# Delta*u*B on GpSimd for some states, and tiles of one state, in a deformable-convolution plus Mamba kernel

## The chip, the cores and the metric

The kernel runs on one core of a Trainium2 chip. A core has TensorE (PE; its weight loads are listed as PEld), VectorE (DVE), ScalarE (ACT), GpSimd (POOL) and SyncE (SP), which here only issues transfers; each works through its own queue in order. On-chip memory is SBUF (128 partitions) and PSUM, which receives the results of TensorE. The metric is the device time of one execution in microseconds.

## The reference

The input is x of shape (4, 128, 128, 128): four images of 128 rows, 128 columns and 128 channels. There are two layers, each `x = x + f(group_norm(x))`.

Layer 0 is a deformable convolution. A 3x3 convolution predicts offsets, each output pixel samples nine shifted positions bilinearly for each of two channel groups, and a depthwise and a pointwise convolution follow.

Layer 1 is a stack of two Mamba blocks. Each image row is a sequence of 128 steps with 128 channels, widened to 256. For each of these 256 channels and 16 states, the block computes a recurrence along the sequence:

```
deltaA  = exp(delta * A)              # decay
deltaBu = (delta * u) * B
h_t     = deltaA_t * h_(t-1) + deltaBu_t
y_t     = sum over the 16 states of h_t * C_t
out     = (y + u * D) * silu(res) @ out_proj
```

u, delta, B and C come from projections of the sequence, a short causal convolution, silu and softplus. All of it is float32.

## The kernel before, in words

Layer 0 works image by image. `gather` issues, on GpSimd, indirect DMAs (L364) that fetch the sampled pixels from a table in device memory, with indices that lie in SBUF; there are 2304 an image. `sample` weights what they brought on DVE (gw, L382, a TENSOR_TENSOR with both inputs in SBUF), adds the samples up on TensorE and copies them to SBUF on ScalarE; `add_up` applies the combined depthwise and pointwise weights on TensorE. Gather buffers (gt) are four deep.

Layer 1 works in jobs: four image rows (`SR`), which are four sequences or 512 steps (`TB`), through one of the two Mamba blocks. An image has 32 such row groups and so 64 jobs. `pre` prepares a job: u, delta, the product du = delta*u (L547 to L550 on DVE), and B and C, which are written to device memory as rows (`bcd`). `main` runs the recurrence. The 256 channels are two halves (`NC`) of 128 partitions, so one state of one job is a tile of 128 x 2 x 512.

In `main`, a step handles two states (`NQ`), and there are eight steps:

- SP loads B and C of the two states, broadcast to all partitions, into `bc0` and `bc1`, two buffers each (L570).
- ScalarE writes zeros to the first step of each sequence in the decay tile `da` (L575), so that the scan starts afresh there, and the decays to the rest (L580, four instructions of 508 elements). There are three `da` tiles.
- DVE makes `hs` = du * B, one instruction per state (L586); then one scan over both states, 2048 elements a partition, which writes the states over the decays in `da` (L592); then the product with C in `da`, also one instruction (L596). The two products are SCALAR_TENSOR_TENSOR with a multiplication by a column of ones.
- TensorE adds the transposed 128x128 pieces into y in PSUM (L128).

After the eight steps DVE multiplies y, in PSUM, with the gate (L607), TensorE projects, and the last block's result goes out through the tile `ot` (L629 to L632).

The main loop runs the steps of layer 1 on image b together with pieces of layer 0 on image b + 1. So the first image's layer 0 runs alone, three images of layer 1 run beside gathers, and the last image of layer 1 runs alone. Each engine's queue has the order that the framework's scheduler gave it from its own estimates of durations and from the free buffers; it is fixed before the run.

Of the kernel before, what the change touches and what calls it, by code (L numbers as in the profile page):

```python
# [10 lines left out]
F32 = mybir.dt.float32  # L11
I32 = mybir.dt.int32
AF = mybir.ActivationFunctionType
ALU = mybir.AluOpType
# [3 lines left out]
P = 128  # L18
G = 2
CG = 64  # L20
NT = 9
RB = 8
SR = 4
TB = SR * P
NGT = 4
NL = 2
NC = 2
NS = 16
NQ = 2
DTR = 8  # L30
DCONV = 4
# [32 lines left out]
def block_kernel(ctx: ExitStack, tc: tile.TileContext, a: dict, out: bass.AP):  # L64
    nc = tc.nc
    x = a["x"]
    B, H, W, C = x.shape
# [21 lines left out]
    cw = ctx.enter_context(tc.tile_pool(name="w", bufs=1))  # L89
# [4 lines left out]
    p2 = ctx.enter_context(tc.tile_pool(name="l1p2", bufs=1))  # L94
# [4 lines left out]
    def loadw(name, shape, src=None, pool=cw, tag=None):  # L99
        t = pool.tile(shape, F32, name=f"w_{name}", tag=tag) if tag else pool.tile(shape, F32, name=f"w_{name}")  # L100
        nc.sync.dma_start(t, a[name] if src is None else src)
        return t
# [13 lines left out]
    ones = cw.tile([P, P], F32, name="ones")  # L116
# [5 lines left out]
    inc = cw.tile([P, NL, DCONV, NC * P], F32, name="inc")  # L122
    aneg = cw.tile([P, NL, NC, NS], F32, name="aneg")
    ddiag = cw.tile([P, NL, NC, P], F32, name="ddiag")

    def add_transposed(o, v, start, stop):

        nc.tensor.matmul(o, v, ident, is_transpose=True, start=start, stop=stop, skip_group_check=True)  # L128
# [4 lines left out]


    dw = loadw("dw", [P, NT, NT], pool=p2, tag="dbl")
    dwb = loadw("dwb", [P, NT], pool=p2, tag="ot")
    pw = loadw("pw", [P, NT, CG], pool=p2, tag="u")
    pwb = loadw("pwb", [P, 1], pool=p2, tag="w1")
    nc.vector.tensor_tensor(
# [15 lines left out]
    alog = loadw("alog", [P, NL, NC, NS], pool=p2, tag="dbl")  # L155
    nc.scalar.activation(aneg, alog, AF.Exp)
    nc.vector.tensor_scalar(aneg, aneg, -1.0, None, ALU.mult)
    dpar = loadw("dpar", [P, NL, NC], pool=p2, tag="ot")
    for l in range(NL):
        for c in range(NC):  # L160
            nc.vector.tensor_scalar(ddiag[:, l, c, :], ident, dpar[:, l, c : c + 1], None, ALU.mult)
    inw = loadw("inw", [P, NL, NC * P], a["inw"][:, :, 0 : NC * P], pool=p2, tag="yg")
    cvw = loadw("cvw", [P, NL, DCONV, NC * P], pool=p2, tag="hs")
    for l in range(NL):
        nc.vector.tensor_tensor(
            inc[:, l], cvw[:, l], inw[:, l].unsqueeze(1).to_broadcast([P, DCONV, NC * P]), ALU.mult
        )


# [289 lines left out]

    NDA = 3
    das = [cw.tile([P, NC, NQ, SR, P], F32, name=f"da{i}") for i in range(NDA)]
    zero = cw.tile([P, NC * NQ * SR], F32, name="zero")
    nc.vector.memset(zero, 0.0)
    n_da = [0]

    NH = 2
# [5 lines left out]
    def next_h():  # L474
        n_h[0] += 1
        return hps[n_h[0] % NH]

    def load_x1(blk, nm):
        b, off = divmod(blk * TB, H * W)
        t = p2.tile([P, TB], F32, tag="x1t", name=f"x1t_{nm}", bufs=2)  # L480
        nc.sync.dma_start(t, x1[b][:, off : off + TB])
        return t
# [70 lines left out]
    def main(st, l):  # L553

        blk = st["blk"]
        nm = f"{blk}_{l}"

        y = psy.tile([P, SR, NC, P], F32, tag="y", name=f"y_{nm}")
        for i in range(SR):
            for c in range(NC):  # L560
                nc.tensor.matmul(  # L561
                    y[:, i, c], st["u"][:, c, i * P : (i + 1) * P], ddiag[:, l, c, :],
                    start=(i % 2 == 0 and c == 0), stop=False, skip_group_check=True,
                )
        for q in range(NS // NQ):
            bc = []
            for w in range(2):
                t = p2.tile([P, NQ, TB], F32, tag=f"bc{w}", name=f"bc{w}_{nm}_{q}", bufs=2)
                n0 = w * NS + q * NQ
                nc.sync.dma_start(t, st["bcd"][n0 : n0 + NQ, :].partition_broadcast(P))  # L570
                bc.append(t)
            da = das[n_da[0] % NDA]
            n_da[0] += 1

            nc.scalar.copy(da.rearrange("p c n s t -> p (c n s) t")[:, :, 0], zero)  # L575
            for c in range(NC):
                dv = st["delta"][:, c].rearrange("p (s t) -> p s t", s=SR)
                for n in range(NQ):
                    s = q * NQ + n
                    nc.scalar.activation(  # L580
                        da[:, c, n, :, 1:], dv[:, :, 1:], AF.Exp, scale=aneg[:, l, c, s : s + 1]
                    )
            hs = p2.tile([P, NC, NQ, TB], F32, tag="hs", name=f"hs_{nm}_{q}")

            for n in range(NQ):
                nc.vector.scalar_tensor_tensor(  # L586
                    hs[:, :, n, :], st["du"], ones[:, 0:1],
                    bc[0][:, n].unsqueeze(1).to_broadcast([P, NC, TB]),
                    op0=ALU.mult, op1=ALU.mult,
                )  # L590
            df = da.rearrange("p c n s t -> p (c n s t)")
            nc.vector.tensor_tensor_scan(  # L592
                df, df, hs.rearrange("p c n t -> p (c n t)"), zero[:, 0:1], ALU.mult, ALU.add
            )
            dc = da.rearrange("p c n s t -> p c (n s t)")
            nc.vector.scalar_tensor_tensor(  # L596
                dc, dc, ones[:, 0:1],
                bc[1].rearrange("p n t -> p (n t)").unsqueeze(1).to_broadcast([P, NC, NQ * TB]),
                op0=ALU.mult, op1=ALU.mult,
            )  # L600
            for c in range(NC):
                for n in range(NQ):
                    for i in range(SR):
                        add_transposed(y[:, i, c], da[:, c, n, i, :], False, q == NS // NQ - 1 and n == NQ - 1)
            yield
        gt = st["g"]
        nc.vector.tensor_tensor(gt, y.rearrange("p s c d -> p s (c d)"), gt, ALU.mult)  # L607
        yg = p2.tile([P, NC, TB], F32, tag="yg", name=f"yg_{nm}")
        for c in range(NC):
            pt = ps1.tile([P, SR, P], F32, tag="t", name=f"pyg_{nm}_{c}")  # L610
            for i in range(SR):
                nc.tensor.transpose(pt[:, i, :], gt[:, i, c * P : (c + 1) * P], ident)  # L612
            nc.scalar.copy(yg[:, c], pt.rearrange("p s t -> p (s t)"))
        po = ps1.tile([P, TB], F32, tag="t", name=f"pout_{nm}")
        if l < NL - 1:
            for c in range(NC):
                nc.tensor.matmul(po, ow[:, l, c, :], yg[:, c], start=(c == 0), stop=(c == NC - 1))
            st["h"] = next_h()
            nc.scalar.copy(st["h"][:, :, DCONV - 1 :], po.rearrange("p (s t) -> p s t", s=SR))
        else:  # L620
            x1t = load_x1(blk, f"o{nm}")
            for i in range(SR):
                o = po[:, i * P : (i + 1) * P]
                nc.tensor.matmul(o, x1t[:, i * P : (i + 1) * P], ident, start=True, stop=False)
                for c in range(NC):
                    nc.tensor.matmul(
                        o, yg[:, c, i * P : (i + 1) * P], ow[:, l, c, :], start=False, stop=(c == NC - 1)
                    )
            ot = p2.tile([P, SR, P], F32, tag="ot", name=f"ot_{nm}")  # L629
            nc.scalar.copy(ot.rearrange("p r c -> p (r c)"), po)  # L630
            b, row = divmod(blk * SR, H)
            nc.sync.dma_start(out[b, row : row + SR].rearrange("r w c -> w r c"), ot)  # L632
# [8 lines left out]
    def layer1():  # L641
        pre(*jobs[0])
        for i, job in enumerate(jobs):
            if i + 1 < len(jobs):
                pre(*jobs[i + 1])
            yield from main(*job)
# [11 lines left out]
    n0 = NJ * NT  # L658
# [67 lines left out]
def build(arrays):  # L726

    import concourse.bacc as bacc

    nc = bacc.Bacc("TRN2", target_bir_lowering=False, num_devices=1)  # L730
    a = {
        k: nc.dram_tensor(f"in_{k}", v.shape, mybir.dt.from_np(v.dtype), kind="ExternalInput").ap()
        for k, v in arrays.items()
    }
    out = nc.dram_tensor("out_0", arrays["x"].shape, F32, kind="ExternalOutput").ap()
    with tile.TileContext(nc) as tc:
        block_kernel(tc, a, out)
    return nc
# [9 lines left out]
```

## Time and profile before

| | us |
|---|---|
| Time, median of 3 runs | 26701.57 (26690.43 to 26703.51) |
| The profiled execution's own time | 26698.06 |
| Its span | 26696.0 |
| DVE busy | 23505.8 (88%) |
| PE busy | 19620.5 (73%) |
| POOL busy | 16017.0 (60%) |
| ACT busy | 11605.1 (43%) |

One profiled execution is taken apart into instructions. A group line gives the kernel line, engine, operation, output tile and inputs, shapes and count; behind the bar stand total busy time in us and the mean of one in ns, then the engine's idle time just before such instructions and what ended it. L128 is a helper, so that its groups are told apart by their tiles. A line of the view by stretches has the stretch and its length, then busy time and number of instructions of each engine, the granted TensorE clock, the share of the DMA engines in use, and GB/s. A line of the timeline has the start, the duration, engine, line and operation, and in brackets the idle time before it and what ended it.

### The profile page before, as it was taken

To read this page: it belongs to the slowest core of one execution; us is meant where nothing else is said; L and a number is where in the kernel's file an instruction comes from. 1 tells how busy PE (TensorE), PEld (TensorE's weight loads), DVE (VectorE), ACT (ScalarE), POOL (GpSimd) and SP (SyncE) were. 2 spreads that over 40 slices of the span, in tenths; PEclk is the share of its full clock that TensorE was granted. 3 is DMA by queue.
4 is the path that set the end of the run, shared out by engine and by line. 5 is a ranking of instruction groups with operands and counts; after the bars stand their busy time and mean duration, and the time that the engine had idled before them with its cause. 6 is when DMAs were issued, how large, how long until landed. Compare 5 with 4: busy or idle time off the path is not lost. (4 is left out here: it accounts for less than half of the span.)

```text
span 26696.0 us, 294801 instructions
## 1 busy us (share of the span) xinstructions
PE 19620.5 (73%) x112196; PEld 13523.4 (51%) x112196; DVE 23505.8 (88%) x14042; ACT 11605.1 (43%) x18181; POOL 16017.0 (60%) x9222
## 2 busy tenths in 40 slices
PE   4777788878888778887888778888888655555555
PEld 3444455555555555555555555555555443434344
DVE  2232289999999999999999999999999999999999
ACT  0000044444444544444444454444445455555554
POOL 4777777878877767888878667877878400000000
PEclk7888888888999888888998888899998866666666
DMA  5363344456544444455544444444444333333332
GB/s 146 114 172 107 106 147 155 157 170 183 165 153 154 149 144 155 158 173 181 164 154 153 148 143 151 156 150 152 154 154 156 130 107 106 107 106 107 107 106 102
DMA packets 1994602, 3804.53 MB, mean 143 GB/s; under 512 B 771796, under 2 KB 1116116, under 8 KB 1993053
## 3 DMA queue, kind: packets, MB, share of 16 engines
q1 hardware_dynamic: 1550812, 2577.13, 29.9%
q0 software_dynamic: 442368, 1208.55, 14.4%
q8 instruction: 880, 14.42, 0.2%
q14 instruction: 542, 4.43, 0.0%
HBM read 3567.63 MB, written 217.05 MB: 142 GB/s over the span
## 5 line engine op out<-in xcount | busy, mean ns | idle before, releaser
L364 POOL DMA_INDIRECT gt<-table,idx x9216 | 16016.3, 1738 | 5031.5 <-issue 2999.5
L592 DVE TENSOR_TENSOR_SCAN da<-da,zero,hs 128x2048 f32<-128x2048 f32 x2048 | 9176.1, 4481 | 351.7 <-ACT da L580 247.1
L128 PE MATMUL y<-ident,da 128*128 128x128 f32 x32768 | 5252.0, 326 | 3956.1 <-DVE da L596 3955.4
L580 ACT ACTIVATE da<-de,aneg 128x508 f32<-128x508 f32 x8192 | 5550.5, 712 | 5605.2 <-PE y L128 5351.0
L128 PEld LDWEIGHTS y<-ident,da 128*128 128x128 f32 x32768 | 4682.4, 171 | 4953.3 <-DVE da L596 2520.6
L415 PE MATMUL acc<-s,wc 128*64 128x256 f32 (+3 forms) x38400 | 6403.2, 453 | 761.4 <-ACT s L396 760.9
L586 DVE SCALAR_TENSOR_TENSOR hs<-du,ones,bc 128x1024 f32<-128x1024 f32 x4096 | 5093.2, 1277 | 0.0
L415 PEld LDWEIGHTS acc<-s,wc 128*64 128x64 f32 x38400 | 3352.0, 145 | 3083.2 <-issue 1446.2
L596 DVE SCALAR_TENSOR_TENSOR da<-da,ones,bc 128x2048 f32<-128x2048 f32 x2048 | 4807.9, 2348 | 25.9
L382 DVE TENSOR_TENSOR gw<-gt,wt 128x1024 f32<-128x1024 f32 x2304 | 2786.4, 1213 | 2133.3 <-DMA gt<-table,idx 1500.9
L128 PE MATMUL p<-ident,gw 128*128 128x128 f32 x18432 | 2724.3, 299 | 1714.1 <-DVE gw L382 1706.7
L128 PEld LDWEIGHTS p<-ident,gw 128*128 128x128 f32 x18432 | 2292.8, 154 | 2329.3 <-DVE gw L382 1752.7
L396 ACT COPY s<-p 128x512 f32<-128x512 f32 x1152 | 668.6, 581 | 3989.8 <-PE p L128 3982.0
L501 PE MATMUL pu<-hp,inc 128*128 128x512 f32 x4096 | 1808.3, 593 | 0.0
L580 ACT ACT_TABLE_LOAD x1016 | 1303.5, 1283 | 16.8 <-PE y L128 5.7
L501 PEld LDWEIGHTS pu<-hp,inc 128*128 128x128 f32 x4096 | 751.2, 188 | 865.9 <-issue 865.2
L508 ACT ACTIVATE u<-pu,w_cvb 128x512 f32<-128x512 f32 x512 | 324.6, 684 | 1468.9 <-PE y L561 1461.4
L561 PEld LDWEIGHTS y<-ddiag,u 128*128 128x128 f32 x4096 | 579.5, 200 | 192.0 <-issue 192.0
L612 PE MATMUL pyg<-ident,g 128*128 128x128 f32 x2048 | 353.9, 328 | 425.7 <-DVE g L607 424.8
L546 ACT ACT_TABLE_LOAD x500 | 641.5, 1283 | 8.9
L561 PE MATMUL y<-ddiag,u 128*128 128x128 f32 x4096 | 612.1, 284 | 0.0
L263 PE MATMUL pof<-xn,w_offw 128*64 128x512 f32 x2304 | 585.0, 613 | 20.0 <-ACT xn L257 12.0
(118 smaller groups left out, 11036.3 us busy)
## 6 DMA issues: line engine op xcount, KB each, us to landing
bc<-bcd SPq DMA_DIRECT2D x4096, 512.0 KB
gt<-table,idx POOLq DMA_INDIRECT x9216
table<-xt SPq DMA_DIRECT2D x984, 128.0 KB
xt<-in_x SPq DMA_DIRECT2D x124, 320.0 KB
xr<-in_x SPq DMA_DIRECT2D x128, 256.0 KB
x<-xo SPq DMA_DIRECT2D x128, 256.0 KB
x1t<-x SPq DMA_DIRECT2D x128, 256.0 KB
x1t_o<-x SPq DMA_DIRECT2D x128, 256.0 KB
```

What stands on the lines that cost most here:

```text
L128: nc.tensor.matmul(o, v, ident, is_transpose=True, start=start, stop=stop, skip_group_check=True)
L364: nc.gpsimd.indirect_dma_start(out=gt[:, v, r], out_offset=None, in_=flat, in_offset=bass.IndirectOffsetOnAxis(ap=idx[:, ri, o : o + 1], a ...
L382: nc.vector.tensor_tensor(gw.rearrange("p r s v c -> p (r s) v c"), gts[h].rearrange("p v r (s c) -> p (r s) v c", c=CG), wv.unsqueeze(3). ...
L396: nc.scalar.copy(st[:, :, 1 : W + 1], p4)
L415: nc.tensor.matmul(accs[b, j + i0][CG * g : CG * g + CG, q : q + rb - ra, :], wc[sl, v, e, :], st[p + 4 * g if p < 4 else 8][sl, ra:rb, kx ...
L501: nc.tensor.matmul(px.rearrange("p (s t) -> p s t", s=SR), inc[:, l, j, c * P : (c + 1) * P], h[:, :, j : j + P], start=(j == 0), stop=(j ...
L546: nc.scalar.activation(du[:, c], w1, AF.Ln)
L561: nc.tensor.matmul(y[:, i, c], st["u"][:, c, i * P : (i + 1) * P], ddiag[:, l, c, :], start=(i % 2 == 0 and c == 0), stop=False, skip_grou ...
L580: nc.scalar.activation(da[:, c, n, :, 1:], dv[:, :, 1:], AF.Exp, scale=aneg[:, l, c, s : s + 1])
L586: nc.vector.scalar_tensor_tensor(hs[:, :, n, :], st["du"], ones[:, 0:1], bc[0][:, n].unsqueeze(1).to_broadcast([P, NC, TB]), op0=ALU.mult, ...
L592: nc.vector.tensor_tensor_scan(df, df, hs.rearrange("p c n t -> p (c n t)"), zero[:, 0:1], ALU.mult, ALU.add)
L596: nc.vector.scalar_tensor_tensor(dc, dc, ones[:, 0:1], bc[1].rearrange("p n t -> p (n t)").unsqueeze(1).to_broadcast([P, NC, NQ * TB]), op ...
```

## The change

One state has tiles of its own now. B of each state is loaded alone into `bs`, three buffers, and C of two states into `cs`, two buffers. There are four decay tiles of one state, set to zero once at the start; ScalarE writes the 127 later steps only, since the scan no longer writes into them. The scan runs over one state, 1024 elements, and writes over `hs`, which has five buffers; the product with C is made in `hs` too.

The product du * B is made by GpSimd for states 0, 4, 8 and 12 in the first three images, and for all states but 7 and 15 in the last image. There DVE's products are TENSOR_TENSOR; in the other images they stay SCALAR_TENSOR_TENSOR.

To make room, the output tile shares the buffer of `w1`, and some weights of the start-up use other tags or come in two loads.

```diff
-    NDA = 3
-    das = [cw.tile([P, NC, NQ, SR, P], F32, name=f"da{i}") for i in range(NDA)]
-    zero = cw.tile([P, NC * NQ * SR], F32, name="zero")
-    nc.vector.memset(zero, 0.0)
+    NDA = 4
+    das = [cw.tile([P, NC, SR, P], F32, name=f"da{i}") for i in range(NDA)]
+    for t in das:
+        nc.vector.memset(t, 0.0)
...
+        last = blk * SR // H == B - 1
+        on_pool = set(range(NS)) - {7, 15} if last else set(range(0, NS, 4))
...
-        for q in range(NS // NQ):
-            bc = []
-            for w in range(2):
-                t = p2.tile([P, NQ, TB], F32, tag=f"bc{w}", name=f"bc{w}_{nm}_{q}", bufs=2)
-                n0 = w * NS + q * NQ
-                nc.sync.dma_start(t, st["bcd"][n0 : n0 + NQ, :].partition_broadcast(P))
-                bc.append(t)
+        for n in range(NS):
+            bs = p2.tile([P, TB], F32, tag="bs", name=f"bs_{nm}_{n}", bufs=3)
+            nc.sync.dma_start(bs, st["bcd"][n : n + 1, :].partition_broadcast(P))
+            if n % NQ == 0:
+                cs = p2.tile([P, NQ, TB], F32, tag="cs", name=f"cs_{nm}_{n}", bufs=2)
+                nc.sync.dma_start(cs, st["bcd"][NS + n : NS + n + NQ, :].partition_broadcast(P))
             da = das[n_da[0] % NDA]
             n_da[0] += 1
-            nc.scalar.copy(da.rearrange("p c n s t -> p (c n s) t")[:, :, 0], zero)
             for c in range(NC):
                 dv = st["delta"][:, c].rearrange("p (s t) -> p s t", s=SR)
-                for n in range(NQ):
-                    s = q * NQ + n
-                    nc.scalar.activation(
-                        da[:, c, n, :, 1:], dv[:, :, 1:], AF.Exp, scale=aneg[:, l, c, s : s + 1]
-                    )
-            hs = p2.tile([P, NC, NQ, TB], F32, tag="hs", name=f"hs_{nm}_{q}")
-            for n in range(NQ):
-                nc.vector.scalar_tensor_tensor(
-                    hs[:, :, n, :], st["du"], ones[:, 0:1],
-                    bc[0][:, n].unsqueeze(1).to_broadcast([P, NC, TB]),
-                    op0=ALU.mult, op1=ALU.mult,
-                )
-            df = da.rearrange("p c n s t -> p (c n s t)")
+                nc.scalar.activation(da[:, c, :, 1:], dv[:, :, 1:], AF.Exp, scale=aneg[:, l, c, n : n + 1])
+            hs = p2.tile([P, NC, TB], F32, tag="hs", name=f"hs_{nm}_{n}", bufs=5)
+            bv = bs.unsqueeze(1).to_broadcast([P, NC, TB])
+            cv = cs[:, n % NQ].unsqueeze(1).to_broadcast([P, NC, TB])
+            if n in on_pool:
+                nc.gpsimd.tensor_tensor(hs, st["du"], bv, ALU.mult)
+            elif last:
+                nc.vector.tensor_tensor(hs, st["du"], bv, ALU.mult)
+            else:
+                nc.vector.scalar_tensor_tensor(hs, st["du"], ones[:, 0:1], bv, op0=ALU.mult, op1=ALU.mult)
+            hf = hs.rearrange("p c t -> p (c t)")
             nc.vector.tensor_tensor_scan(
-                df, df, hs.rearrange("p c n t -> p (c n t)"), zero[:, 0:1], ALU.mult, ALU.add
+                hf, da.rearrange("p c s t -> p (c s t)"), hf, 0.0, ALU.mult, ALU.add
             )
-            dc = da.rearrange("p c n s t -> p c (n s t)")
-            nc.vector.scalar_tensor_tensor(
-                dc, dc, ones[:, 0:1],
-                bc[1].rearrange("p n t -> p (n t)").unsqueeze(1).to_broadcast([P, NC, NQ * TB]),
-                op0=ALU.mult, op1=ALU.mult,
-            )
+            if last:
+                nc.vector.tensor_tensor(hs, hs, cv, ALU.mult)
+            else:
+                nc.vector.scalar_tensor_tensor(hs, hs, ones[:, 0:1], cv, op0=ALU.mult, op1=ALU.mult)
             for c in range(NC):
-                for n in range(NQ):
-                    for i in range(SR):
-                        add_transposed(y[:, i, c], da[:, c, n, i, :], False, q == NS // NQ - 1 and n == NQ - 1)
-            yield
+                for i in range(SR):
+                    add_transposed(y[:, i, c], hs[:, c, i * P : (i + 1) * P], False, n == NS - 1)
+            if n % NQ == NQ - 1:
+                yield
...
-            ot = p2.tile([P, SR, P], F32, tag="ot", name=f"ot_{nm}")
+            ot = p2.tile([P, SR, P], F32, tag="w1", name=f"ot_{nm}")
```

More of the change, by code (lines that the diff above doesn't have):

```diff
@@ L135, in block_kernel @@
     dw = loadw("dw", [P, NT, NT], pool=p2, tag="dbl")
-    dwb = loadw("dwb", [P, NT], pool=p2, tag="ot")
+    dwb = loadw("dwb", [P, NT], pool=p2, tag="yg")
     pw = loadw("pw", [P, NT, CG], pool=p2, tag="u")
@@ L157, in block_kernel @@
     nc.vector.tensor_scalar(aneg, aneg, -1.0, None, ALU.mult)
-    dpar = loadw("dpar", [P, NL, NC], pool=p2, tag="ot")
+    dpar = loadw("dpar", [P, NL, NC], pool=p2, tag="u")
     for l in range(NL):
@@ L162, in block_kernel @@
     inw = loadw("inw", [P, NL, NC * P], a["inw"][:, :, 0 : NC * P], pool=p2, tag="yg")
-    cvw = loadw("cvw", [P, NL, DCONV, NC * P], pool=p2, tag="hs")
     for l in range(NL):
+        cvw = p2.tile([P, DCONV, NC * P], F32, tag="hs", name=f"w_cvw_{l}", bufs=5)
+        nc.sync.dma_start(cvw, a["cvw"][:, l])
         nc.vector.tensor_tensor(
-            inc[:, l], cvw[:, l], inw[:, l].unsqueeze(1).to_broadcast([P, DCONV, NC * P]), ALU.mult
+            inc[:, l], cvw, inw[:, l].unsqueeze(1).to_broadcast([P, DCONV, NC * P]), ALU.mult
         )
```

## The prediction

> **What bounds the kernel now.** I read the page first: engine totals, costliest groups, then busy time by stage, and last two stretches of the timeline.
>
> ```profile
> span 26696.0 us, 294801 instructions
> PE 19620.5 (73%) x112196; PEld 13523.4 (51%) x112196; DVE 23505.8 (88%) x14042; ACT 11605.1 (43%) x18181; POOL 16017.0 (60%) x9222
> L364 POOL DMA_INDIRECT gt<-table,idx x9216 | 16016.3, 1738 | 5031.5 <-issue 2999.5
> L592 DVE TENSOR_TENSOR_SCAN da<-da,zero,hs 128x2048 f32<-128x2048 f32 x2048 | 9176.1, 4481 | 351.7 <-ACT da L580 247.1
> L586 DVE SCALAR_TENSOR_TENSOR hs<-du,ones,bc 128x1024 f32<-128x1024 f32 x4096 | 5093.2, 1277 | 0.0
> L596 DVE SCALAR_TENSOR_TENSOR da<-da,ones,bc 128x2048 f32<-128x2048 f32 x2048 | 4807.9, 2348 | 25.9
> ```
>
> Three groups of VectorE (DVE) make 19,077 us of its 23,506: the scan, the product delta*u*B (L586) and the product with C (L596). The next view is busy time by stretch: one image with gathers, then the last image, which has none.
>
> ```profile
> 8900.00:14900.00 6000.00, 4792.57 (x28204) 3299.27 (x28201) 5873.82 (x3523) 2892.36 (x4563) 4621.39 (x2323) 0.89 0.50 159
> 20900.00:26696.00 5796.00, 3073.34 (x14161) 2350.39 (x14157) 5495.89 (x2718) 2918.84 (x4443) 110.16 (x56) 0.70 0.31 107
> ```
>
> The columns are PE, PEld, DVE, ACT, POOL. DVE is busy 98% and 95%: it sets the time in both. GpSimd (POOL) is busy 77% beside gathers and idle in the last image; ScalarE and TensorE have room. The third view is the timeline of the two engines in one gather stretch:
>
> ```profile
> 10013.81 0.95 POOL L364 DMA_INDIRECT gt<-table,idx  x1 [0.30 <-issue]
> 10015.06 0.95 POOL L364 DMA_INDIRECT gt<-table,idx  x1 [0.30 <-issue]
> 10016.31 5.13 POOL L364 DMA_INDIRECT gt<-table,idx  x1 [0.30 <-issue]
> 10021.74 0.94 POOL L364 DMA_INDIRECT gt<-table,idx  x1 [0.30 <-issue]
> ...
> 10038.55 4.16 POOL L364 DMA_INDIRECT gt<-table,idx  x1 [0.30 <-issue]
> ```
> ```profile
> 10015.07 1.23 DVE L607 TENSOR_TENSOR g<-y,g 128x1024 f32<-128x1024 f32 x1 [1.25 <-PE y L128]
> 10016.21 4.48 DVE L592 TENSOR_TENSOR_SCAN da<-da,zero,hs 128x2048 f32<-128x2048 f32 x1
> 10020.60 1.20 DVE L382 TENSOR_TENSOR gw<-gt,wt 128x1024 f32<-128x1024 f32 x1
> ...
> 10037.47 4.48 DVE L592 TENSOR_TENSOR_SCAN da<-da,zero,hs 128x2048 f32<-128x2048 f32 x1
> ```
>
> These lines carry my forecast. A gather issue takes 0.95 us, also beside L607, one of whose inputs is in PSUM. The issue that meets a scan takes 5.13: the scan ends at 10020.69, the issue at 21.44, 0.75 later. The second shows the same: 41.95 against 42.71. GpSimd reads its indices from SBUF and stands still while DVE runs an instruction with two SBUF inputs; the scan itself keeps its 4.48.
>
> **The change part by part.** The sum is made against the profiled execution's own 26,698 us (span 26,696 and 2 around it), 4 under the median shown, 26,702.
>
> (a) Tiles of one state. Two sizes of the same operation give its fixed part: 2 x 1277 - 2348 = 206 ns. 2048 products with C become 4096: 2048 x 206 ns = 422 us more. The scan has one size only; with the same fixed part half of it is (4481 - 206) / 2 + 206 = 2344 ns, again 422 us. Bounds: a fixed part of 72 ns (a one-column DVE memset, the smallest DVE row) gives 147 us for the scan; 412 ns, twice mine, 844. I take 206 because the scan lies in the same stream of instructions. Together +844 us, all on the path.
>
> (b) delta*u*B off DVE. Images 0 to 2 have 64 jobs each (32 row blocks x 2 layers) with 4 states moved, the last 64 with 14: 768 + 896 = 1664 instructions. A row of L586 costs 5093.2 / 4096 = 1243 ns net of overlaps, so -2069 us.
>
> (c) In the last image the 64 x 16 products with C and the 64 x 2 products left become TENSOR_TENSOR: 1214 ns (L607, same size) for 1277, 1152 x 63 ns = -73 us.
>
> DVE alone: 844 - 2069 - 73 = -1298 us; by image, 211 - 318 = -107 in each with gathers, 211 - 1114 - 73 = -976 in the last.
>
> (d) The 1664 products on GpSimd. No such row exists. The nearest are its own: memsets of one column, 98 to 119 ns (108), and the one-input affine select of 128x128, 286. So (286 - 108) / 127 = 1.40 ns an element; 1024 elements are 1.54 us in one pass. Two inputs lie between one pass and two: 1.54 to 2.98 us, and as both must be read I take the middle, 2.26. What this costs the path has two ends. Low end: none, since nothing in this trace has GpSimd reading for microseconds, and it may run beside DVE. High end: GpSimd and DVE exclude each other. Scan, product with C, remaining product and L382 all have two SBUF inputs, the kind beside which the index read stood still. Then each product displaces DVE for its length less about 0.21, the fixed part of a DVE instruction that may pass under it: 2.05 us, 1664 x 2.05 = +3411 us. I take the high end: the only reads by GpSimd that this trace has were stopped to the end of the DVE instruction. Whether DVE stops GpSimd or the reverse matters little, for the next scan needs that product anyway. With 1.54 and 2.98 it is +2213 and +4609.
>
> What a page says weighs against this change. The Trainium skill, "SBUF — State Buffer", section "Who interferes with whom", states that a DVE instruction with two SBUF inputs contends with a GpSimd instruction that reads SBUF, and that the later one blocks fully. The blocked issues above agree for a short read; no row here shows a long one. The same skill, "GPSIMD Engine Reference", section 3.1, measures 4497 ns for a two-input operation on 2048 elements; half, 2.25 us, is an estimate from that page and would make 28,795 us, against 25,400 if no port were shared.
>
> (e) GpSimd's queue. A product waits there for its broadcast of B, for du (L550) and for a free hs buffer; the gathers behind it wait too, and behind them DVE's L382. Beside gathers an image has 2304 issues x (1993 + 300) ns = 5283 us, and 256 x 2.26 = 579 makes 5862 of 6000: it just fits. Where each product also sits out a half scan (2.34 us), it is 6461, and GpSimd becomes the bound.
>
> (f) At nothing: 2048 zero copies leave ScalarE (427.9 us; it is 43% busy, and DVE waited 247 us in all for its decays). Four decay tiles, freed by the scan instead of by TensorE, let ScalarE run three states ahead, as against one tile of two now; if that cover fails, it is those 247 us again. SP issues 4096 B tiles and 2048 C tiles in place of 4096, with the same bytes; its waits are mostly for L596 (13,472 us), so it runs ahead; three B buffers reach three states, over 10 us. If a transfer were late, GpSimd would stand still first. The output tile shares w1's buffer: ScalarE may wait for a store, with half its time free. Start-up edits are a few us.
>
> Sum: 26,698 - 1298 + 3411 = 28,811, said as 28,800 us.
>
> **Rivals.**
> 1. (0.53) Products and DVE instructions exclude each other, as above: 28,811, from 27,613 (one pass) to 30,009 (two).
> 2. (0.32) They run side by side: 25,400, up to 26,400 with late gathers and decays. For it: the stopped part of an issue is one index read, perhaps handled otherwise than a streamed operand; a scan takes 2.09 ns an element (half its 4481 ns less 206, over 1024) where the product takes 1.05, so it may leave half of the reads free. Against: the issues that end 0.75 us behind a scan. Decision point: 1298 / 1664 = 0.78 us of DVE time lost for each product; below it the kernel gains.
> 3. (0.12) GpSimd is slowed to about 4.6 us a product (2.26 + 2.34) while DVE is not. In the last image 14 x 4.6 = 64 us fit in the job's 5209 - 976 = 4233 us / 64 = 66; beside gathers it is short by 461 us an image: 26,698 - 976 + 3 x 461 = 27,105, from 26,200 to 27,600. For it: GpSimd has only 23% free there. Against: it now sits idle 682 us of a 6000 us stretch waiting for DVE to free gather buffers.
> 4. (0.03) Gain and loss cancel within 0.2%, about what a measurement here can tell from no change.
>
> (The 5209 is 64 jobs of the last image: 8 x (4481 + 2 x 1277 + 2348) + 2 x 678 + 2 x 682 + 1216 + 1208 + 1214 ns = 81.4 us each.)
>
> **How the numbers follow.** Slower: rival 1 whole and 0.07 of rival 3, 0.60; faster: rival 2 and 0.05 of rival 3, 0.37; same 0.03. The likeliest case gives 28,800, by itself 27,600 to 30,000. The other sign has over a third, so the range goes from 25,400 (0.08 below it: waits in DVE that vanish) to 29,900 (0.10 above).
>
> **What would show it.** Right: the scan or product with C stretched from their 2.3 and 1.2 us towards 4 to 5, or idle in front of scans put down to GpSimd's hs; GpSimd products of over 4 us with ends just behind DVE instructions; a last image of about 6.4 ms in place of 5.5. Wrong: scans at 2.34 us without gaps beside GpSimd products, and DVE shorter by 1.3 ms. For (a): scan mean other than 2344 ns, product other than 1277. For rival 3: idle before L382 put down to gathers. The forecast goes wrong most simply if GpSimd's streamed reads are not held like its index reads.

## The result, and the profile after

The changed kernel takes 29,141 us (29,136.6 to 29,143.9); measured beside it, the kernel before takes 26,696. The ratio is 1.092, 95% interval 1.091 to 1.093: slower, as forecast, by 2445 us where 2100 were forecast.

The page of the changed kernel, engine totals and the groups that answer to those shown of before. Lines have moved by one or two: the scan is L594, the products with B are L588 (GpSimd), L590 and L592 (DVE), those with C L598 (last image) and L600, the weighting of gathered pixels L383.

```profile
span 29134.7 us, 301116 instructions
PE 19924.6 (68%) x112196; PEld 13697.5 (47%) x112196; DVE 24020.9 (82%) x16477; ACT 11101.7 (38%) x15941; POOL 19259.8 (66%) x10886
L365 POOL DMA_INDIRECT gt<-table,idx x9216 | 14286.0, 1550 | 6170.4 <-DVE gw L383 3177.5
L594 DVE TENSOR_TENSOR_SCAN hs<-da,hs 128x1024 f32<-128x1024 f32 x4096 | 9821.1, 2417 | 2406.5 <-POOL hs L588 2404.6
L588 POOL TENSOR_TENSOR hs<-du,bs 128x1024 f32<-128x1024 f32 x1664 | 4973.1, 2995 | 3673.5 <-PE y L128 2928.2
L592 DVE SCALAR_TENSOR_TENSOR hs<-du,ones,bs 128x1024 f32<-128x1024 f32 x2304 | 3064.9, 1349 | 61.6 <-PE y L128 61.0
L598 DVE TENSOR_TENSOR hs<-hs,cs 128x1024 f32<-128x1024 f32 x1024 | 2059.5, 2035 | 2.2
L600 DVE SCALAR_TENSOR_TENSOR hs<-hs,ones,cs 128x1024 f32<-128x1024 f32 x3072 | 4087.5, 1344 | 2.8
```

Two things stand out. DVE lost 1664 instructions and is busy longer than before (24,021 us against 23,506): the product with C in the last image takes 2035 ns where TENSOR_TENSOR of this size took 1214. And DVE stands idle 2405 us in front of scans, waiting for GpSimd's product; that wait did not exist.

Busy time of DVE by image shows that the two belong to different places. Each line is one image of layer 1 on DVE: three beside gathers and the last. The bounds are the first scan and the ends of the 64th, 128th, 192nd and 256th product with the gate (one a job); columns are the stretch, its length, DVE's busy time and instructions, the granted clock, DMA share and GB/s. First the kernel before, then the changed one:

```profile
3471.00:9470.00 5999.00, 5863.50 (x3540) 0.89 0.50 160
9470.00:15435.00 5965.00, 5838.26 (x3502) 0.89 0.50 159
15435.00:21356.00 5921.00, 5761.03 (x3348) 0.88 0.46 150
21356.00:26685.00 5329.00, 5057.92 (x2487) 0.69 0.31 106
```
```profile
3482.00:10075.00 6593.00, 5839.52 (x4269) 0.85 0.47 144
10075.00:16680.00 6605.00, 5839.21 (x4274) 0.85 0.47 144
16680.00:23244.00 6564.00, 5786.91 (x4151) 0.84 0.44 136
23244.00:29123.00 5879.00, 5567.51 (x2616) 0.65 0.29 96
```

Beside gathers an image is some 625 us longer with DVE no busier: it waits. The last image is 550 us longer with DVE 510 us busier: its instructions take longer. How, the timeline of the last image shows, DVE and then GpSimd:

```profile
25991.26 3.30 DVE L590 TENSOR_TENSOR hs<-du,bs 128x1024 f32<-128x1024 f32 x1
25994.48 1.21 DVE L598 TENSOR_TENSOR hs<-hs,cs 128x1024 f32<-128x1024 f32 x1
25995.62 8.72 DVE L594 TENSOR_TENSOR_SCAN hs<-da,hs 128x1024 f32<-128x1024 f32 x2
...
26008.72 1.19 DVE L607 TENSOR_TENSOR g<-y,g 128x1024 f32<-128x1024 f32 x1
26009.83 2.19 DVE L598 TENSOR_TENSOR hs<-hs,cs 128x1024 f32<-128x1024 f32 x1
```
```profile
25994.95 2.95 POOL L588 TENSOR_TENSOR hs<-du,bs 128x1024 f32<-128x1024 f32 x1 [1.48 <-DMA bs<-bcd]
25998.08 4.11 POOL L588 TENSOR_TENSOR hs<-du,bs 128x1024 f32<-128x1024 f32 x1 [0.17 <-DMA bs<-bcd]
26007.56 3.38 POOL L588 TENSOR_TENSOR hs<-du,bs 128x1024 f32<-128x1024 f32 x1 [5.37 <-PE y L128]
```

The two engines take turns. GpSimd's product of 25994.95 comes while DVE is in L598, which ends at 25995.69, and ends 2.21 us behind that, at 25997.90. The first of DVE's two scans starts at 25995.62, and the pair takes 8.72 us; an undisturbed pair takes 4.46. The product of 26007.56 ends at 26010.94; the L598 that starts at 26009.83 takes 2.19 and ends 1.08 behind it. L607, one of whose inputs is in PSUM, keeps its 1.19 beside the same product. Over the last image, of the L598 that started while a product ran, the median ended 1083 ns behind the product's end, where an L598 alone takes 1212 in all. L549, with an input in PSUM, took 678 ns alone and 679 beside a product, while L548, whose inputs are both in SBUF, took 676 alone and 2759.

### The profile page after: what moved, and what is told of

Read it like the earlier page. It is cut to its first block, busy times and chain, and to the rows that moved or that the text cites. A ratio compares the mean times of both kernels' runs of the same rounds, so it can differ in the third digit from the quotient of the medians.

```text
span 29134.7 us, 301116 instructions
## 1 busy us (share of the span) xinstructions
PE 19924.6 (68%) x112196; PEld 13697.5 (47%) x112196; DVE 24020.9 (82%) x16477; ACT 11101.7 (38%) x15941; POOL 19259.8 (66%) x10886
## 4 chain that ended last, share of the span: by engine, by line
POOL 36%; issue 34%; DVE 21%; PE 4%; DMA 3%; ACT 1%; SPq 1%; DVEq 0%; POOLq 0%; ACTq 0%
POOL gt L365 30%; DVE hs L594 8%; POOL hs L588 6%; DVE hs L598 3%; DVE hs L592 3%; DMA gt<-table,idx 2%; DVE hs L600 2%; DVE gw L383 1%; PE pdb L522 1%; DVE e L548 1%; PE acc L416 1%; DVE hs L590 1%; PE y L128 1%; DVE de L550 1%; ACT da L581 1%
## 5 line engine op out<-in xcount | busy, mean ns | idle before, releaser
L365 POOL DMA_INDIRECT gt<-table,idx x9216 | 14286.0, 1550 | 6170.4 <-DVE gw L383 3177.5
L594 DVE TENSOR_TENSOR_SCAN hs<-da,hs 128x1024 f32<-128x1024 f32 x4096 | 9821.1, 2417 | 2406.5 <-POOL hs L588 2404.6
L128 PE MATMUL y<-ident,hs 128*128 128x128 f32 x32768 | 5284.3, 324 | 4854.3 <-DVE hs L598 2848.3
L588 POOL TENSOR_TENSOR hs<-du,bs 128x1024 f32<-128x1024 f32 x1664 | 4973.1, 2995 | 3673.5 <-PE y L128 2928.2
L128 PEld LDWEIGHTS y<-ident,hs 128*128 128x128 f32 x32768 | 4572.5, 169 | 5902.8 <-DVE hs L598 3069.2
L383 DVE TENSOR_TENSOR gw<-gt,wt 128x1024 f32<-128x1024 f32 x2304 | 3046.5, 1329 | 2011.1 <-DMA gt<-table,idx 1385.3
L600 DVE SCALAR_TENSOR_TENSOR hs<-hs,ones,cs 128x1024 f32<-128x1024 f32 x3072 | 4087.5, 1344 | 2.8
L592 DVE SCALAR_TENSOR_TENSOR hs<-du,ones,bs 128x1024 f32<-128x1024 f32 x2304 | 3064.9, 1349 | 61.6 <-PE y L128 61.0
L598 DVE TENSOR_TENSOR hs<-hs,cs 128x1024 f32<-128x1024 f32 x1024 | 2059.5, 2035 | 2.2
L581 ACT ACT_TABLE_LOAD x920 | 1180.4, 1283 | 37.0 <-DVE hs L594 21.1
L514 PE MATMUL pr<-w_resw,hp 128*128 128x256 f32 x2048 | 609.3, 450 | 516.7 <-ACT u L509 516.5
L522 PE MATMUL pdb<-u,w_xpw 128*41 128x512 f32 x1024 | 710.3, 833 | 295.3 <-ACT g L519 295.1
```

The lines of the kernel that those rows point to most:

```text
L365: nc.gpsimd.indirect_dma_start(out=gt[:, v, r], out_offset=None, in_=flat, in_offset=bass.IndirectOffsetOnAxis(ap=idx[:, ri, o : o + 1], a ...
L383: nc.vector.tensor_tensor(gw.rearrange("p r s v c -> p (r s) v c"), gts[h].rearrange("p v r (s c) -> p (r s) v c", c=CG), wv.unsqueeze(3). ...
L522: nc.tensor.matmul(pdb[0:XP], xpw[:, l, c, :], u[:, c], start=(c == 0), stop=(c == NC - 1))
L581: nc.scalar.activation(da[:, c, :, 1:], dv[:, :, 1:], AF.Exp, scale=aneg[:, l, c, n : n + 1])
L588: nc.gpsimd.tensor_tensor(hs, st["du"], bv, ALU.mult)
L592: nc.vector.scalar_tensor_tensor(hs, st["du"], ones[:, 0:1], bv, op0=ALU.mult, op1=ALU.mult)
```

## The experiments

Each kernel was compared with the kernel before on the same chip. Experiments 1 to 4, 9 and 10 ran on chips where the kernel before takes some 26,700 us, as on the first one, 5 to 8 on one where it takes 27,321 us. Times in the text are medians.

**1 to 3. No product on GpSimd; only in the last image; only beside gathers.** One line of the changed kernel each:

```diff
-        on_pool = set(range(NS)) - {7, 15} if last else set(range(0, NS, 4))
+        on_pool = set()                                            # e1
+        on_pool = set(range(NS)) - {7, 15} if last else set()      # e2
+        on_pool = set() if last else set(range(0, NS, 4))          # e3
```

> The changed kernel with no product on GpSimd: tiles of one state alone. Theory 1 (GpSimd products and DVE instructions with two SBUF inputs exclude each other, each product displaces DVE by about 2.2 us): 26698 + 844 (split) - 56 - 73 less most of the 247 us of waits for decays, 27,200 to 27,450 us, and scans at about 2280 ns with no idle put down to GpSimd. Rival A (the split itself is what costs: shorter tiles, more waits between them): 28,500 us or more. Rival B (GpSimd's waits for free hs buffers, 2928 us, and DVE's waits for GpSimd, 2405 us, are the cost, not the port): also about 27,300, since there is nothing left to wait for.

> GpSimd makes 14 of 16 products in the last image only, none beside gathers. Theory 1: each of 896 products takes 2.2 us from DVE and saves it 1.1, so the time with no product on GpSimd plus about 1000 us: 28,200 to 28,500. Rival C (products hold up the gathers behind them, which is where the loss lies): within 200 us of the kernel with none.

> GpSimd makes every fourth product beside the gathers, none in the last image. Theory 1: 768 products, each 2.2 us less 1.24 saved, so the time with none plus about 750 us: 28,000 to 28,250; and with the one above the two excesses add up to the changed kernel's 29,141 within 150 us. Rival C: most of the excess is here, 1500 us or more.

Measured, beside 26,702 for the kernel before: e1 26,307 (ratio 0.985, 0.984 to 0.987), e2 27,178 (1.018, 1.016 to 1.020), e3 28,277 (1.059, 1.057 to 1.061). The excesses over e1, 871 and 1970 us, add up to 29,148; the changed kernel has 29,141. So the two places are independent, and what is left of the change (e1) costs nothing.

The absolute times that I had expected were too high for e1 (27,200 to 27,450) and e2 (28,200 to 28,500), because the kernel with no product on GpSimd came some 1000 us lower than I took it; e3 came close to its 28,000 to 28,250 only because its excess was 1200 us larger than theory 1's.

Rival A falls, and with it a term of the forecast: the kernel with tiles of one state is not slower but faster than the kernel before. e1's page shows how, and below it are its second and its last image:

```profile
PE 19515.8 (74%) x112196; PEld 13544.1 (52%) x112196; DVE 23515.8 (89%) x18141; ACT 11159.7 (42%) x15975; POOL 14295.8 (54%) x9222
L594 DVE TENSOR_TENSOR_SCAN hs<-da,hs 128x1024 f32<-128x1024 f32 x4096 | 9222.7, 2274 | 6.5 <-DVE hs L592 0.5
```
```profile
9428.00:15374.00 5946.00, 5888.34 (x4530) 0.88 0.53 160
21271.00:26287.00 5016.00, 4933.90 (x3511) 0.67 0.37 113
```

4099 more DVE instructions, and the same busy time within 10 us; the scan's 351.7 us of idle before it, mostly for decays, are 6.5. DVE's idle over the span falls by 408 us (3190 to 2782).

Per product the last image loses 871 / 896 = 0.97 us, near theory 1's 1.1. Beside gathers it is 1970 / 768 = 2.57, not the 1.0 of theory 1: rival C has the better of it there. The waits of DVE in e3 (total us, times, longest) and its second image:

```profile
DVE hs L594 <- POOL hs L588: 2096.1, 415, 14.4
DVE gw L383 <- DMA gt<-table,idx: 1380.3, 386, 16.8
```
```profile
10094.00:16695.00 6601.00, 5842.50 (x4274) 0.85 0.48 144
```

The first line accounts for the excess of e3; the second, which stood at 1370 in e1, belongs to the first image's gathers.

**4. GpSimd writes without reading.** At the same places in its queue, on the same tiles, with the same waits for a free tile, three zero writes instead of a product. B and du are not read, so that the waits for them fall away too.

```diff
-                nc.gpsimd.tensor_tensor(hs, st["du"], bv, ALU.mult)
+                for _ in range(3):
+                    nc.gpsimd.memset(hs, 0.0)
```

> In place of each of the 1664 products GpSimd writes zeros over the tile three times (0.108 + 1024 x 0.79 ns = 0.92 us each by the start-up memsets, 2.8 us together, no less than the product's 2.26 us undisturbed); so du*B of these states is left out of the result. The waits for a free hs buffer, the place in GpSimd's queue and DVE's wait for the tile stay; only the reads of SBUF are gone. Theory 1: DVE runs undisturbed, 25,300 to 25,900 us, below the kernel before. Rival B (waits on buffers and queue): 28,500 us or more, as in the changed kernel. Between 26,500 and 28,000 both have a share.

Measured 27,597 us (1.034, 1.032 to 1.036): between the two. Lines have moved by one more: the scan is L595, the product with C of the last image L599. By image, DVE again:

```profile
3487.00:10078.00 6591.00, 5603.41 (x4275) 0.85 0.47 144
10078.00:16661.00 6583.00, 5600.82 (x4275) 0.85 0.47 144
16661.00:23178.00 6517.00, 5524.94 (x4145) 0.85 0.44 137
23178.00:27584.00 4406.00, 3931.91 (x2617) 0.71 0.41 128
```

In the last image both theories get a plain answer. Buffers and queue are as before, GpSimd writes for 2.9 us a state (958 ns a write), and the image takes 4406 us instead of 5879, with DVE busy for 3932 instead of 5568; DVE's L599, the product with C, has a median of 1215 ns beside the writes and without. So it is GpSimd's reads that stop DVE, and they cost this image 1473 us, 1.64 for each of 896 products. GpSimd's waits for free buffers (1939 us in this image) cost little: DVE waits 461 us for its tiles here.

Beside gathers the answer is the other one: 6583 us, the same as with products, though DVE is no longer slowed (busy 5601 instead of 5839). So at this place in the queue it makes no difference to the time what GpSimd does. DVE waits for these tiles in the three images:

```profile
DVE hs L595 <- POOL hs L589: 2668.9, 492, 15.0
```

**5, 6 and 10. Products issued earlier, beside gathers only.** The timeline of the changed kernel shows the place in the queue, first GpSimd, then DVE:

```profile
12007.80 2.69 POOL L365 DMA_INDIRECT gt<-table,idx  x1 [4.12 <-DVE gw L383]
12010.79 0.95 POOL L365 DMA_INDIRECT gt<-table,idx  x1 [0.30 <-issue]
...
12021.24 0.95 POOL L365 DMA_INDIRECT gt<-table,idx  x1 [0.30 <-issue]
12022.21 2.37 POOL L588 TENSOR_TENSOR hs<-du,bs 128x1024 f32<-128x1024 f32 x1
```
```profile
12006.31 1.22 DVE L383 TENSOR_TENSOR gw<-gt,wt 128x1024 f32<-128x1024 f32 x1
12009.65 1.20 DVE L383 TENSOR_TENSOR gw<-gt,wt 128x1024 f32<-128x1024 f32 x1
...
12018.85 2.45 DVE L600 SCALAR_TENSOR_TENSOR hs<-hs,ones,cs 128x1024 f32<-128x1024 f32 x2
12024.62 2.29 DVE L594 TENSOR_TENSOR_SCAN hs<-da,hs 128x1024 f32<-128x1024 f32 x1 [3.32 <-POOL hs L588]
```

GpSimd stands at a gather whose buffer is not free until DVE's L383 has read it. Then it issues the eight gathers of one unit, 14.4 us, some of them stopped by scans, and only then comes the product that DVE's next scan needs. DVE runs dry at 12021.3 and waits 3.32 us. In e5 the states 3, 7, 11 and 15 are GpSimd's, with two buffers of their own; two products are issued at the start of the job and each further one when an earlier one is used up. To make room there are three `hs` and two `bs` buffers.

```diff
+        on_pool = [] if last else [3, 7, 11, 15]
+        made = {}
+        def product():
+            n = on_pool.pop(0)
+            bp = p2.tile([P, TB], F32, tag="bp", name=f"bp_{blk}_{l}_{n}", bufs=2)
+            nc.sync.dma_start(bp, st["bcd"][n : n + 1, :].partition_broadcast(P))
+            made[n] = p2.tile([P, NC, TB], F32, tag="hp", name=f"hp_{blk}_{l}_{n}", bufs=2)
+            nc.gpsimd.tensor_tensor(made[n], st["du"], bp.unsqueeze(1).to_broadcast([P, NC, TB]), ALU.mult)
+        for _ in on_pool[:2]:
+            product()
...
+            if n in made and on_pool:
+                product()
```

e6 has the three zero writes in place of the product, e10 the product on DVE (scalar_tensor_tensor).

> As the kernel with products on GpSimd beside the gathers only (28,277), with the same number of products, but each one is issued four states or more before its scan (states 3, 7, 11, 15; two buffers of their own, and the first two at the start of the job), so that a burst of eight gathers ahead of it in GpSimd's queue has time to pass. Theory Q (beside gathers the loss is the product's place behind gathers that wait for DVE's weighting): DVE's waits for GpSimd's products fall from 2096 us to under 300, and what is left is the exclusion at the port: an image has DVE 5885 - 318 + 256 x 2.06 = 6094 us, about 6150 with its idle, against 6590; in all 26,307 + 3 x 220 = 26,970 us (26,700 to 27,200). Rival P (port alone, in any order, or a GpSimd that is simply full): 28,000 to 28,300.

> The same with three zero writes for each product, so du*B of these states is left out of the result; no reads by GpSimd. Theory Q with the port: DVE undisturbed, an image at 5885 - 318 + about 70 of idle = 5640 us; 26,307 - 3 x 290 = 25,440 (25,300 to 25,800). The difference to the kernel above, about 1500 us over 768 products, is then the port's share beside gathers, 2 us each. If the place in the queue does not matter: 28,000 or more.

> Control for the kernels with products issued ahead: the same tiles, buffers and order of issue (three hs buffers, two B buffers, two for states 3, 7, 11, 15), the products of these states made by DVE. An image beside gathers has DVE busy 5890 and the waits that the fewer buffers bring, some 150 to 300 us: 6,050 to 6,200 us, above the 5,920 with zero writes on GpSimd and below the 6,500 with products on GpSimd. So with the queue's place loosened a product on GpSimd still loses about 1.2 us (2.3 taken, 1.2 saved). If it came out at 6,450 or more, the buffers, not GpSimd, would explain the time of the kernel with products issued ahead.

On the other chip e5 takes 29,055 us beside 27,321 (1.064, 1.062 to 1.065), e6 27,281 (0.998, 0.997 to 0.999). e10 ran on one like the first: 26,889 beside 26,701 (1.007, 1.005 to 1.009). On the other chip layer 1 starts at 4085 to 4106 us instead of 3471 to 3491, about the 620 us by which the kernel before differs, so I compare images of layer 1, not totals. The last image, the same code in all three, takes 5446, 5448 and 5445 us. The second image of each, in the order e5, e6, e10:

```profile
10629.00:17136.00 6507.00, 6036.72 (x4275) 0.85 0.48 146
```
```profile
10033.00:15955.00 5922.00, 5594.76 (x4275) 0.89 0.54 160
```
```profile
9501.00:15505.00 6004.00, 5892.20 (x4531) 0.88 0.52 158
```

DVE's waits for what GpSimd makes, e6 and then e5, and below them two more waits of e5, SP's and DVE's (L566 loads B for a product made ahead, L568 is that product, L607 is here DVE's own product with B):

```profile
DVE hp L610 <- POOL hp L569: 567.1, 147, 11.4
```
```profile
DVE hp L609 <- POOL hp L568: 190.5, 52, 5.7
SPq L566 <- POOL hp L568: 6494.3, 688, 25.1
DVE hs L607 <- DMA bs<-bcd: 596.5, 130, 12.5
```

With zero writes the earlier place takes an image from 6583 to 5922 us, and DVE's waits for GpSimd from 2669 us to 567: the place in the queue was worth over 600 us an image, as theory Q says. With products DVE's waits for them fall too, from 2096 us to 190, but the image gains only 94 us (6601 to 6507). DVE's idle falls from 759 to 470 us, while its busy time rises from 5843 to 6037: what the earlier place gains, the exclusion takes back in large part. e5 less e6 is 585 us an image, of which 442 are longer busy time of DVE, 1.73 for each of 256 products.

My totals were missed all the same. e5 ended 1734 us above its kernel before, where 26,970 would have been 270 above and rival P's 28,000 to 28,300 some 1300 to 1600. The exclusion alone, as in rival P, does not explain e4, which loses as much without reads. e6's image is 5922 and not 5640 us, in part since 567 us of waits for the tiles remain in all. The last image, without any product, is 430 us above e1's 5016 in all three, with 390 us of waits for TensorE to free `hs`: the price of fewer buffers. Beside gathers that price is small, 6004 us in e10 against 5946 in e1.

Against e10 each product on GpSimd in e5 loses (6507 - 6004) / 256 = 1.96 us, 1.2 by my expectation. The chips differ, but in these two images DVE waits for no gather. The rest has a second queue in it: the load of B for a product made ahead (L566) stands in SP's queue until GpSimd has freed its buffer, 6494 us in all, and DVE's tiles of B and C are loaded behind it. In one case SP issues this load at 12048.71, when the product of 12046.32 has ended, and four loads of B and C behind it by 12051.37; DVE, dry since 12045.4, goes on at 12057.73. In e6, where the zero writes read no B, SP stands there 460 us, in e10 1753, for DVE. In the second image DVE waits 247 us for tiles of B and C in e5, 8 in e6 and 12 in e10, with the same buffers in all three. Less these waits the loss is (503 - 235) / 256 = 1.05 us a product, near the expected 1.2. So part of the wait has only moved, from DVE's own wait for GpSimd to SP's.

**9. One read in place of two**, in the last image only; the factor B is left out of these states.

```diff
-                nc.gpsimd.tensor_tensor(hs, st["du"], bv, ALU.mult)
+                nc.gpsimd.tensor_copy(hs, st["du"])
```

> As the kernel with 14 of 16 products on GpSimd in the last image only, but GpSimd copies du into the tile, one input from SBUF in place of two, and so leaves the factor B out of these states. If the exclusion goes by GpSimd's reads and lasts as long as they do, the last image lies between that with zero writes (4407 us) and that with products (5880): by the affine select, 1.54 us for one pass less 0.2, 4407 + 896 x 1.3 = 5,600 us, and DVE instructions with two SBUF inputs that start during a copy end about 1.08 us (product with C) or 2.15 us (scan) behind the copy's end. If only instructions with two inputs exclude DVE: about 4,400.

Measured 26,097 us (0.977, 0.976 to 0.979). The last image:

```profile
21289.00:26080.00 4791.00, 4498.57 (x2617) 0.70 0.37 118
```

DVE instructions that start during a copy end 1074 ns (L598) and 2139 ns (scan) behind it: the exclusion needs no second input on GpSimd's side. A copy is shorter than I took from the affine select: begun during L598, it ends 0.90 us behind it, where a product ends 2.2 behind. The image loses (4791 - 4406) / 896 = 0.43 us a copy against zero writes, a product 1.64. DVE's busy time rises by 567 us with copies, 0.63 each, and by 1636 with products, 1.83 each; its idle time, 474 us with zero writes, falls to 292 and 311, about 0.2 each. Some of the turns of 0.90 and 2.2 us fall beside L607 and L549, which they do not stop; how many was not counted. The forecast of 5,600 us for this image was 800 too high.

**7 and 8. A version without GpSimd.** e7 is the kernel before with the one thing of the change that helped, in two-state tiles:

```diff
-    NDA = 3
+    NDA = 2
...
-            nc.scalar.copy(da.rearrange("p c n s t -> p (c n s) t")[:, :, 0], zero)
...
-            hs = p2.tile([P, NC, NQ, TB], F32, tag="hs", name=f"hs_{nm}_{q}")
+            hs = p2.tile([P, NC, NQ, TB], F32, tag="hs", name=f"hs_{nm}_{q}", bufs=2)
...
+            nc.vector.tensor_tensor_scan(
+                hf, da.rearrange("p c n s t -> p (c n s t)"), hf, 0.0, ALU.mult, ALU.add
+            )
```

Its product with C works on `hs`, and the last image has TENSOR_TENSOR. e8 has TENSOR_TENSOR in all images.

> The kernel before with only one thing of the change: the scan writes over hs (two buffers of two states), so that the decay tiles (two, of two states) keep their zeros and ScalarE writes none; nothing on GpSimd; TENSOR_TENSOR in the last image. If the 395 us that the kernel with no product on GpSimd gains over before come from the decays no longer being waited for, this has them too, and saves the split of the product with C, 246 us: 25,950 to 26,350. If they come from the smaller tiles, or two decay tiles bring the waits back: 26,500 to 26,700.

> The same with TENSOR_TENSOR for both products in all images: 3072 + 1536 instructions 63 ns shorter, 290 us less than the one above, 25,650 to 26,050, if the gathers still come in time (GpSimd now waits some 1,170 us an image for DVE). Rival: gathers stand still longer, because the short start of the three-operand form no longer lets them in, and DVE waits for what they bring: the time of the one above or more.

Both ran on the chip of e5. e7 takes 27,939 us (1.022, 1.021 to 1.024), e8 28,731 (1.051, 1.050 to 1.053): both slower than before, where I had expected faster. In e7 the waits for decays are gone, but others are there: DVE's products wait 465 and 188 us for TensorE to free one of the two `hs` tiles. So with two tiles of two states keeping the zeros gains nothing; e1's gain came with five and four small buffers in place of few large ones. That buffers are the whole reason was not tried apart.

e8 confirms its rival. The group of GpSimd's gathers, e7 and then e8:

```profile
L365 POOL DMA_INDIRECT gt<-table,idx x9216 | 15981.7, 1734 | 6394.3 <-DVE gw L383 3252.0 <-issue 2928.7 <-DVE fi L291 72.5
```
```profile
L365 POOL DMA_INDIRECT gt<-table,idx x9216 | 18434.9, 2000 | 4769.6 <-issue 3009.9 <-DVE gw L383 1556.2 <-DVE fi L291 116.9
```

And DVE's waits for them (total us, times, longest), in the same order:

```profile
DVE gw L383 <- DMA gt<-table,idx: 307.0, 56, 17.0
```
```profile
DVE gw L383 <- DMA gt<-table,idx: 1346.5, 371, 17.0
```

DVE's products are some 63 ns shorter and the gathers 266 ns longer, and DVE waits 1040 us more for what they bring.

The version that beats both kernels and leaves nothing out is e1: the change's tiles, nothing on GpSimd, 1.5% faster than before.

## Why the prediction was right, and where it was not

The forecast was 28,800 us for the case of mutual exclusion; measured is 29,141, in its own range and on its side. The mechanism is shown for the last image. But that the total came within 350 us is partly luck, since its errors went both ways. By its terms the kernel without products on GpSimd should have been 715 us above before, the products of the last image should have cost 780 and those beside gathers 620; measured are -395, 871 and 1970. One error of 1110 us too much stands against one of 1350 too little.

**(a) Tiles of one state, +844 us: wrong.** With (c) it should have made +715 without GpSimd; e1 shows -395. The working took 206 ns of fixed part from two durations. Durations of neighbours on DVE overlap by some 80 ns in the trace (before, an L596 of 2.35 us starts at 10021.72 and its successor at 10023.99), as (b) allowed for and (a) did not; and the scan hardly has a fixed part: 2274 ns for half of 4481, 67 ns a pair where I took 207. The product with C went from 4808 us to 5054, +246 instead of +422; TENSOR_TENSOR in the last image is some 60 of the difference. All in all DVE's busy time stayed.

**(f) At nothing: wrong on the good side.** The 247 us of waits for decays vanished, and DVE's idle fell by 408 us in all. I named the reason, decay tiles freed by the scan, and gave it no value.

**(b) -2069 us for 1664 products off DVE: about right.** With zero writes in their place, DVE is busy 21,648 us against e1's 23,516: -1868, or 1.12 us each instead of 1.243.

**(d) Exclusion, 2.05 us a product: right in kind and nearly in size in the last image.** A product that starts during L598 or a scan ends 2.2 or 2.1 us behind it; 2.26 was taken. It costs that image 1.64 us against zero writes: 1.83 of longer DVE instructions less 0.18 of idle that goes.

The rule of the Trainium skill ("SBUF — State Buffer", "Who interferes with whom") holds here in both directions and in both its conditions. In the runs, DVE instructions with two SBUF inputs stretched (1212 to 3305 ns for L598), those with one in PSUM did not (L549, 678 and 679), and GpSimd's writes stopped nobody (L599, 1215 ns). The 2.25 us worked out from "GPSIMD Engine Reference", section 3.1, an estimate, was 0.1 below the 2.36 us that products took which started beside no DVE instruction.

One reading behind (d) was too wide: GpSimd's index read does not stand still beside every DVE instruction with two SBUF inputs. The gather of 10021.74, shown in the prediction, took 0.94 us although this L596, with two SBUF inputs, ran beside it:

```profile
10021.72 2.35 DVE L596 SCALAR_TENSOR_TENSOR da<-da,ones,bc 128x2048 f32<-128x2048 f32 x1
```

**(e) GpSimd's queue, "it just fits": the step that failed.** I weighed whether GpSimd had enough time in an image; it had, and is idle 3178 us waiting for L383 over the run. The cost lay in the order: a product that DVE waits for stood behind gathers that wait for DVE. I had listed who waits behind a waiting product, but not what the product itself stands behind. Beside gathers that is 2.57 us a product where the terms had 0.81 (2.05 less 1.24), and zero writes at the same place take as long as products (6583 and 6605 us an image). There the exclusion is hidden behind the queue and shows only when products are issued earlier (e5 against e6).

**Rivals.** Rival 2, side by side, would have been 25,400; the last image with zero writes, 4406 us, is what it would have looked like there (5329 - 976 = 4353). Rival 3 named the right place, the queue beside gathers, for a wrong reason, too little time. Its last image, unharmed, is refuted.

## What to carry to other kernels

Moving work off the bound engine does not help while the work still needs what that engine is bound by. Here nearly all of DVE's work reads two SBUF operands, and GpSimd's reads shut exactly these out: a product that costs DVE 1.2 us holds it up for up to 2.2 us on GpSimd, 1.8 on average in the last image. And before putting work that the bound engine waits for into the queue of a helper, look at what stands in front of it: behind eight gathers that themselves wait for the bound engine, even zero writes, which stopped no DVE instruction, cost 2.5 us a tile (6583 against 5946 us in e1, 256 tiles). Issued earlier, the task can make the load queue wait instead, as e5 shows.

## What was not expected of the hardware

- GpSimd's reads and DVE's instructions with two SBUF inputs exclude each other from both sides, for a whole instruction: an L598 that starts during a product ends 1083 ns behind its end, a product that starts during L598 ends 2.2 us behind it. Instructions with one input in PSUM are not held. A copy of one operand does the same for 0.90 us; 1024-element writes of 0.96 us do not.
- The form of a DVE instruction bears on how gathers fare between such instructions. In the kernel before, of the gathers issued within 26 ns of the start of a product with a column of ones, all took 0.94 to 0.96 us, as if alone (528 at L596, 1160 at L586). Of 66 issued as close to the start of TENSOR_TENSOR L382, 55 took 2.0 us. It is not the operation's name: L302 is a SCALAR_TENSOR_TENSOR too, with a constant where the products have the column, and 11 gathers at its start took 3.3 us each. With TENSOR_TENSOR everywhere the mean gather went from 1734 to 2000 ns (e7, e8).
- The same program takes 620 us longer on another chip. In the kernels that ran there, the first image's 2304 gathers take the same 1040 ns each, but GpSimd stands idle 1283 to 1314 us between them instead of 702, before layer 1 begins.
